# Products of constants, read by nobody, placed in TensorE's waits: routed FFN fronts, experts' first rows, layer 1 and the mixers' fronts

## The chip, the core and the metric

The kernel runs on one core of a Trainium2 chip. The time is device microseconds from start to end of one execution. A profiled execution also gives a trace with a record of each instruction of the engines: TensorE (PE), with its weight loads apart (PEld), VectorE (DVE), ScalarE (ACT), GpSimd (POOL) and SyncE (SP), which issues DMAs here. It also gives PEclk, the clock that the throttle granted to TensorE, as a share of full speed.

## The reference

A net of four layers works on `x` of shape [2, 512, 256] in FP32, that is 1024 tokens of width 256. Each layer is a feed-forward part, a mixing part and a second feed-forward part with the same weights, each added to `x` after a layernorm.

```python
# L0 ffn: 32 experts, top 6, plus a shared expert
scores = softmax(x2d @ wg_router.T); topk_w, topk_idx = top_k(scores, 6)
...
g = einsum('ecd,edf->ecf', xe, w_gate); u = einsum('ecd,edf->ecf', xe, w_up)
ye = einsum('ecf,efd->ecd', silu(g) * u, w_down)
...
return y + silu(x2d @ ws_gate) * (x2d @ ws_up) @ ws_down
```

Layer 0 mixes by retention (followed by an MLP), layer 1 by sparse attention between two binarized linear layers, layer 2 by a Mamba2 block with 8 heads, layer 3 by one with 64 heads. Layer 2's feed-forward part has 8 dense experts, of which each token takes one. Layer 3's is routed like layer 0's, with 8 experts, of which each token takes 2. So the routed feed-forward part runs four times: twice in layer 0, twice in layer 3.

## The kernel before

`x` stays in SBUF as 8 chunks of 128 tokens, four to each half `b`. The stages run one after the other (list at L2083). A tile framework orders the instructions of each engine by a simulated list schedule, and gives PSUM slots out of pools: a tile with the tag `mm` takes a slot of the pool when the earlier owner has been read. `in_order` (L136 to L153) pins the program order of the engines that it names, within its block. What a stage leaves for `x` is added late: `self.pending[b]` holds a function for each chunk, which `settle` calls.

**Routed feed-forward, `moe` (L621 to L722).** The front (L646 to L660) does for each half a layernorm on DVE and GpSimd (L208 to L223), then 8 transposes on PE (`transpose_tokens`, L172 to L178, two PSUM tiles of 512 columns). After both halves come the router's `logits` (L312 to L321: for each chunk two accumulated matmuls of 32 or 8 columns), copied out by DVE at L320; then the scores (L730 to L735 in layer 0, L748 in layer 3), top k and slot lists on DVE (L299 to L307, `slot_lists` L403 to L503). PE and ACT are pinned in the front. The shared expert (`shared_unit`, L355 to L393) follows on PE in the meantime: `pg` and `pu` (L365), `Silu` on ACT (L368), `h` on DVE (L369), the product back (L375) and the addition to `x` (L393).

**Experts, `experts_sparse` (L506 to L616).** The work is a pipeline over units (expert and up to two tiles of 128 rows). GpSimd gathers rows by an indirect DMA (L527), `turn_x` transposes them (L541) and evacuates them into `xeT`, `hidden` multiplies by gate and up (L551, 352 columns) and forms `he` (L555 on ACT, L556 on DVE), `turn_h` transposes (L565), `down_` multiplies (L576), and GpSimd scatters the result to DRAM (L581). A second such loop sits in a branch (L690 to L692) that runs only when an expert has more rows than its tiles; the trace shows it not taken.

**Layer 1 (L1105 to L1440).** A loop at L1301 runs over chunks with stages `front`, `turn_x`, `back`, `measure`, `norm`. `front` begins with the addition of what layer 0 left: six rows per token are read back from DRAM (`add_rows`, L696 to L722) and summed on PE against the identity (L711).

**Mamba, `mamba` (L1567 on).** Its head (L1946 to L2001) pins PE, ACT and DVE. `row(0)` makes the first half's transposed layernorm; in layer 3 it runs chunk by chunk (`by_chunks`, L254 to L276): add the pending rows, normalise one chunk, two transposes (L272). In layer 2, named `few` in the code, the rows are there at once. Then `decay_sums` (L1606 to L1672: `pd` at L1620, row sums `ps_row` L1646, `ps_cum` L1664, `ps_dec` L1669), projections with a convolution (`pp` L1679, ACT L1682, taps on DVE L1686), `products` of B and C (L1703 to L1716) and `prep_back` (L1758 to L1765).

## Time and profile before

| | us |
|---|---|
| median of 3 runs | 2017.6 |
| lowest, highest | 2016.25, 2018.17 |
| the profiled execution | 2018.74 |
| its span, first to last instruction | 2016.9 |
| its mean granted clock of TensorE | 0.923 |

The page's idle times tell for how long an engine stood still before an instruction and which engine's end or DMA released it. For example, the ACT line among the waits

```
ACT s L368 <- PE pg L365: 47.9, 13, 8.8
```

says that ACT stood still before `s` (L368) 13 times for `pg` from PE, 47.9 us in all and 8.8 at the longest. A window line (a stretch in us) gives the busy time and the number of instructions of PE, PEld, DVE, ACT and POOL, then the granted clock, the share of the DMA engines and GB/s. In the slices of the page each digit is a tenth.

TensorE is 87% busy over the span. It stands still at the seams of the stages, where the next layernorm, a gather or rows from DRAM come first.

### The profile page before, as it was taken

How to read it: one execution, taken by the hardware profiler on the slowest of the kernel's cores; microseconds unless marked ns; L12 is line 12 of the kernel's file. 1: busy time of each engine (PE TensorE's matmuls, PEld its weight loads, DVE VectorE, ACT ScalarE, POOL GpSimd, SP SyncE). 2: the span in 40 equal slices, each digit the busy share in tenths (PEclk: the TensorE clock that was granted, in tenths of full speed). 3: DMA queues.
4: the chain of work that ended last, by engine and by line, in shares of the span. 5: the costliest groups of instructions: out<-in, count | busy, mean ns of one | idle time of the engine just before them, and what ended most of it. 6: DMA issues, size and time to landing. Idle time of an engine off the chain costs nothing. (4 is left out here: it accounts for less than half of the span.)

```text
span 2016.9 us, 29547 instructions
## 1 busy us (share of the span) xinstructions
PE 1748.0 (87%) x10566; PEld 1243.7 (62%) x10566; DVE 1145.4 (57%) x2673; ACT 796.8 (40%) x1340; POOL 903.6 (45%) x889
## 2 busy tenths in 40 slices
PE   6899769788999678789788989589999899999885
PEld 4677636465777545454465457357777677777564
DVE  4433276226333376556584643478777787777533
ACT  1123224311233134301661012268777677777111
POOL 3477655310777430100140026136657456767253
PEclk9899989888999889979897989699999999999788
DMA  8266440050556600000230013434454444543133
GB/s 312 82 189 190 147 178 12 11 167 13 170 185 185 214 27 1 2 21 1 95 106 22 3 54 98 137 123 149 152 168 147 147 147 159 172 149 118 44 97 96
DMA packets 117439, 226.47 MB, mean 112 GB/s; under 512 B 22382, under 2 KB 68828, under 8 KB 117014
## 3 DMA queue, kind: packets, MB, share of 16 engines
q1 hardware_dynamic: 88134, 170.17, 25.8%
q0 software_dynamic: 20608, 48.45, 7.5%
q10 hardware_dynamic: 8528, 5.72, 0.9%
q8 instruction: 92, 1.51, 0.3%
q14 instruction: 77, 0.63, 0.1%
HBM read 195.59 MB, written 41.81 MB: 118 GB/s over the span
## 5 line engine op out<-in xcount | busy, mean ns | idle before, releaser
L527 POOL DMA_INDIRECT xe<-table,sl_get x176 | 180.3, 1024 | 211.1 <-DVE sl_get L503 122.0
L551 PE MATMUL ps_gu<-we,xeT 128*128 128x352 f32 x704 | 234.2, 476 | 3.1 <-DVE xeT L130 3.1
L581 POOL DMA_INDIRECT rows<-ye,sl_put x176 | 176.8, 1005 | 82.7 <-issue 41.4
L1686 DVE SCALAR_TENSOR_TENSOR xc<-pp,L_attn_cols,xc 128x511 f32<-128x511 f32 (+2 forms) x216 | 161.4, 747 | 28.7 <-ACT xc L1682 23.4
L576 PE MATMUL ps_ye<-we,hT 88*128 88x256 f32 x704 | 168.1, 379 | 2.9 <-ACT ye L132 1.7
L556 DVE SCALAR_TENSOR_TENSOR he<-se,xe,ps_gu 128x176 f32<-128x176 f32 x176 | 69.9, 397 | 176.1 <-ACT se L555 167.0
L551 PEld LDWEIGHTS ps_gu<-we,xeT 128*128 128x128 f32 x704 | 130.8, 197 | 62.1 <-issue 6.0
L576 PEld LDWEIGHTS ps_ye<-we,hT 88*128 88x128 f32 x704 | 133.4, 190 | 36.5 <-ACT ye L132 3.6
L1813 PE MATMUL pz<-xT,wt 128*128 128x128 f32 x1152 | 143.3, 278 | 12.4 <-ACT xt L1762 6.2
L1789 DVE SCALAR_TENSOR_TENSOR lm<-lm,jb,top 128x128 f32<-128x128 f32 x576 | 153.6, 341 | 0.0
L1679 PE MATMUL pp<-xT,wx 128*128 128x512 f32 x288 | 143.2, 621 | 4.8 <-issue 1.6
L1813 PEld LDWEIGHTS pz<-xT,wt 128*128 128x128 f32 x1152 | 135.9, 193 | 17.8 <-issue 9.3
L555 ACT ACTIVATE se<-ps_gu 128x176 f32<-128x176 f32 x176 | 55.8, 317 | 228.2 <-PE ps_gu L551 228.2
L1898 PE MATMUL yacc<-wt,y 128*128 128x256 f32 x576 | 143.0, 391 | 0.9 <-POOL y L1868 0.6
L1868 POOL TENSOR_TENSOR y<-y,sg 128x512 f32<-128x512 f32 x72 | 91.8, 1274 | 106.3 <-DVE y L1867 104.8
L1806 POOL TENSOR_TENSOR ce<-ce,CT 128x1024 f32<-128x1024 f32 x54 | 127.9, 2369 | 0.0
L1898 PEld LDWEIGHTS yacc<-wt,y 128*128 128x128 f32 x576 | 104.0, 190 | 23.7 <-issue 10.1
L1518 PE MATMUL ps_y<-w8T,xT 128*128 128x512 f32 x256 | 118.4, 617 | 0.0
L1841 PE MATMUL py<-lm,xt 128*64 128x128 f32 x1152 | 108.2, 282 | 10.6 <-DVE lm L1798 3.9
L1798 DVE TENSOR_TENSOR lm<-lm,M 128x1024 f32<-128x1024 f32 x72 | 87.2, 1215 | 46.7 <-ACT lm L1794 44.1
L1879 POOL TENSOR_TENSOR sqs<-sqs,sq 128x512 f32<-128x512 f32 x56 | 71.3, 1274 | 89.0 <-ACT sq L1878 89.0
L217 POOL TENSOR_SCALAR ln_rstd<-ln_mv 128x4 f32<-128x4 f32 x15 | 3.5, 235 | 234.9 <-DVE ln_mv L209 223.7
(402 smaller groups left out, 3465.3 us busy)
## 6 DMA issues: line engine op xcount, KB each, us to landing
lm<-rows SPq DMA_DIRECT2D x72, 512.0 KB
ce<-rows SPq DMA_DIRECT2D x54, 512.0 KB
rows<-zero POOLq DMA_DIRECT2D x16, 768.0 KB, 9.4
y<-rows SPq DMA_DIRECT2D x16, 768.0 KB
we<-in_L_ffn_w_gate_dram SPq DMA_DIRECT2D x64, 176.0 KB
we<-in_L_ffn_w_up_dram SPq DMA_DIRECT2D x64, 176.0 KB
we<-in_L_ffn_w_down_dram SPq DMA_DIRECT2D x64, 176.0 KB
we<-in_L_ffn_w_dram SPq DMA_DIRECT2D x48, 176.0 KB
```

Source lines behind the costliest of these rows:

```text
L527: nc.gpsimd.indirect_dma_start(xe[:, i, :], None, table, bass.IndirectOffsetOnAxis(get[:, e * per + j : e * per + j + 1], 0), bounds_check ...
L551: nc.tensor.matmul(pg, xeT[:, k, i * P : (i + 1) * P], wgu[:, :, k], start=(k == 0), stop=(k == KD - 1))
L576: nc.tensor.matmul(py[:, i, :], hT[:, q, i * P : (i + 1) * P], wd[:, q, :], start=(q == 0), stop=(q == 1))
L581: put_rows = nc.gpsimd.indirect_dma_start(rows, bass.IndirectOffsetOnAxis(put[:, e * per + j : e * per + j + 1], 0), y[:, i, :], None, bou ...
L1518: nc.tensor.matmul(ps, xT[:, k, cs], self.w8T[:, k, 2 * e2 : 2 * e2 + 2, :], start=(k == 0), stop=(k == KD - 1))
L1679: nc.tensor.matmul(pp, wv[:, k, :], xT[:, k, b * S : (b + 1) * S], start=(k == 0), stop=(k == KD - 1))
L1686: nc.vector.scalar_tensor_tensor(out[:, 3 - w :], pp[:, : S - 3 + w], cw[:, m, w : w + 1], out[:, 3 - w :], ALU.mult, ALU.add)
L1789: nc.vector.scalar_tensor_tensor(k["lm"][:, h, :], k["lm"][:, h, :], jb[:, k["c"], n : n + 1], top, ALU.add, ALU.min)
L1806: nc.gpsimd.tensor_tensor(k["ce"], k["ce"], ct, ALU.mult)
L1813: nc.tensor.matmul(pz[:, m, :], u["wz"][:, kk, m * P : (m + 1) * P], xT[:, kk, c * P : (c + 1) * P], start=(kk == 0), stop=(kk == KD - 1),)
L1841: nc.tensor.matmul(py[i * HP : (i + 1) * HP, m, :], w[:, h * HP : (h + 1) * HP], v[:, h, :], start=(m == 0 and n == 0), stop=(n == len(src ...
L1898: nc.tensor.matmul(yacc[cc // 2][:, cc % 2, :], k["y"][:, m, :], u["wo"][:, m, :], start=(u["g"] == 0 and m == 0 and cc % 2 == 0), stop=(u ...
```

## The change

A helper `warm(psum, n)` takes one PSUM tile and multiplies the identity n times by 256 columns of a constant table into it. Nobody reads the tile. The calls, with the number of products:

- `moe` front: 4 ahead of each half, and 1 after each of the first 7 chunks of the logits (15 in each of the four fronts)
- `experts_sparse`: 2 ahead of the transposes of the first unit's rows and 2 after them, in the slot of the second unit's down product (so `down_` now names its tag; the slot is the same)
- `by_chunks`: 1 ahead of each of the first 3 chunks' transposes
- layer 1: 18 ahead of the loop
- `decay_sums(0)`: 4 ahead of the row sums; `products(0)`: 4 ahead; `prep_back` of the first unit, m = 2: 3 ahead
- `mamba` front: 4 in layer 2, 18 in layer 3, ahead of `row(0)`

In the code of the calls that run, this is 60 + 16 + 3 + 18 + 8 + 8 + 6 + 22 = 141 products. The branch of L690 has its own four, which don't run.

```diff
+    def warm(self, psum, n, tag="mm", w=256):
+        ps = psum.tile([P, S], F32, tag=tag, name="warm")
+        for _ in range(n):
+            self.nc.tensor.matmul(ps[:, :w], self.ident, self.c["le"][:, :w], start=True, stop=True)
...
@@ by_chunks
                     self.centre(xn[:, j, :], b * CB + j, *ms[j])
+                    if j < CB - 1:
+                        self.warm(psum, 1)
                     for k in range(KD):
...
@@ logits
-    def logits(self, pool, psum, xT, wT, e):
+    def logits(self, pool, psum, xT, wT, e, warm=False):
...
+            if warm and c < NC - 1:
+                self.warm(psum, 1)
         self.nc.vector.tensor_copy(lg, ps)
...
@@ experts_sparse
         def turn_x(n, xe, nt):
+            if n == 0:
+                self.warm(ps, 2, tag="ps_ye1")
             pt = ps.tile([P, KD, nt * P], F32, name="ps_xe")
...
+            if n == 0:
+                self.warm(ps, 2, tag="ps_ye1")
             xeT = ew.tile([P, KD, nt * P], F32, name=f"xeT{n % 2}")
...
-            py = ps.tile([P, nt, D], F32, name=f"ps_ye{n % 2}")
+            py = ps.tile([P, nt, D], F32, tag=f"ps_ye{n % 2}", name=f"ps_ye{n % 2}")
...
@@ moe
                         for b in range(B):
+                            self.warm(psM, 4)
                             xn = lp.tile([P, CB, D], F32, name=f"xn{b}")
...
-                        s = self.logits(sb, psM, xT, rT, E)
+                        s = self.logits(sb, psM, xT, rT, E, warm=True)
...
@@ l1
             with tc.tile_pool(name="a1m", bufs=4, space=PSUM) as psM:
+                self.warm(psM, 18)
                 for c in range(NC + 4):
...
@@ mamba: decay_sums, products, prep_back, head
                 yield
+                if b == 0:
+                    self.warm(psM, 4)
...
             def products(b):
+                if b == 0:
+                    self.warm(psM, 4)
...
             def prep_back(u, m):
+                if u["b"] == u["g"] == 0 and m == 2:
+                    self.warm(psM, 3)
...
             with self.in_order(tail, ("PE", "Activation", "DVE")):
+                self.warm(psM, 4 if few else 18)
                 row(0)
```

## The prediction

> **What bounds the kernel now.** I read the busy shares first, then the slices with the granted clock, then windows of 3.41 us, then the timeline around each place that the change touches.

> From the page, parts 1 and 2:

> ```profile
> PE 1748.0 (87%) x10566; PEld 1243.7 (62%) x10566; DVE 1145.4 (57%) x2673; ACT 796.8 (40%) x1340; POOL 903.6 (45%) x889
> ...
> PE   6899769788999678789788989589999899999885
> ...
> PEclk9899989888999889979897989699999999999788
> ```

> TensorE is the bound over the whole, but with gaps at the seams between stages, and behind the gaps the granted clock falls. The mean clock is 0.923; since the record only ever shows 1.0 and 0.5, about 15% of the span, some 310 us, is at half clock, much of it idle. The change can only win where matmuls run at half clock on the path.

> Next, windows that follow the clock's own grid (columns: stretch in us; busy us and instruction count of PE, PEld, DVE, ACT, POOL; granted clock; DMA share; GB/s):

> ```profile
> 441.84:445.25 3.41, 2.16 (x8) 1.48 (x8) 2.53 (x9) 0.00 (x0) 0.74 (x1) 0.50 0.09 33
> 452.08:455.50 3.42, 3.42 (x18) 3.42 (x18) 0.00 (x0) 0.88 (x1) 0.00 (x0) 0.50 0.60 207
> 458.91:462.32 3.41, 3.41 (x5) 1.35 (x4) 1.64 (x11) 1.61 (x2) 0.00 (x0) 0.50 0.00 0
> 462.32:465.74 3.42, 3.42 (x9) 1.52 (x8) 2.51 (x13) 0.60 (x1) 0.00 (x0) 1.00 0.00 0
> 503.28:506.70 3.42, 1.19 (x6) 0.63 (x5) 2.24 (x6) 0.00 (x0) 2.70 (x3) 1.00 0.72 211
> 506.70:510.11 3.41, 2.63 (x6) 1.54 (x6) 2.33 (x4) 0.00 (x0) 2.60 (x3) 0.50 0.45 137
> ```

> Busy time does not lift the clock: the second window is 100% busy with router logits (32 columns each) and stays at half; one window of 512-column matmuls (458.91) lifts it. In the fifth, PE is busy 1.19 of 3.42 us and the clock falls at its end. I counted, for every window of the trace, the share in which columns stream (columns times 1.67 ns at half clock: 256 columns take 0.427 us there and 0.216 at full). Of windows at half clock those at 0.61 to 0.64 stayed, 0.71 and 0.75 mostly rose; of those at full clock, the ones below about 0.3 mostly fell, those from 0.35 up mostly stayed.

> Then the timeline (start, us, engine, line, operation, out<-in, count, idle before and its releaser):

> ```profile
> 449.92 6.88 PE L317 MATMUL ps_lg<-routerT,xT 128*128 128x32 f32 x32
> 456.61 3.76 PE L365 MATMUL pg<-xT,wsh 128*128 128x512 f32 x4
> 463.23 0.69 DVE L369 SCALAR_TENSOR_TENSOR h<-s,pu 128x512 f32<-128x512 f32 x1 [2.58 <-PE pu L365]
> ...
> 506.30 0.72 PE L541 MATMUL ps_xe<-cst,xe 128*128 128x128 f32 x3 [0.92 <-DMA xe<-table,sl_get]
> 507.81 5.06 PE L551 MATMUL ps_gu<-we,xeT 128*128 128x352 f32 x8 [0.78 <-DVE xeT L130]
> ...
> 1161.09 4.09 PE L317 MATMUL ps_lg<-routerT,xT 128*128 128x8 f32 x32
> ...
> 1278.08 0.66 PE L272 MATMUL ps_tr<-cst,xn 128*128 128x128 f32 x2 [13.24 <-DVE xn L198]
> 1283.90 3.68 PE L1620 MATMUL pd<-wb,xT 128*128 128x64 f32 x16 [0.57 <-DVE xT L130]
> ```

> A front (449.92) runs logits and its first 512-column products at half clock, and DVE then waits for them. The first expert's matmul (507.81) takes 5.06 us; the same eight instructions at 519.95 take 2.53. Layer 3's mixer idles 13.24 us and starts cold.

> [...] the clock changes only at multiples of 3.41 us. [...] window 441.84 (8 transposes, 2.16 us busy) stayed at 0.50. [...] the trace has two instructions for each matmul call (32 for the 16 calls of the logits), so I count one added product as two instructions of 256 columns.

> **The change part by part.** It removes nothing and adds 141 executed products = 282 instructions: 60.9 us of PE at 0.216, 120 us at 0.427. Each site is worth what it shortens behind it, less what it delays. Waits for a PSUM slot I put at nothing: no reader holds a product's tile, the logits hold one of the four slots while the products rotate over the other three, the chunks of the mixer's front hold two, and the slot that the first rows take is not used before the second unit's down product. If such a wait came, it would stand in PE's queue ahead of the transposes or logits; a product ahead of it lasts 0.43 to 0.86 us, so that is its bound per site.

> *First expert rows* (four times: two products before the transposes of x, two after). Layer 0: the first gather waits leave PE near idle, and the evacuation gap (0.78 us) holds two products (0.86) almost entirely. If the clock stays up, the eight instructions take 2.53 instead of 5.06: +2.95 us in the first, +2.8 in the second call. GpSimd, whose gathers and scatters run nearly without pause there (4 x 1.32 us a unit against PE's 5.0), has caught up with 4.9 us to spare by the loop's end, so the gain passes through. Layer 3: PE waits 5.06 us for the gather (1198.98), longer than a window, and two products fill only 0.86 of it; eight instructions from 1200.87 at 0.62 each; I take +0.8 each (-0.3 to +1.4), because with more columns in the window the clock should rise 3.4 us earlier in part of the phases. Sum +7.3.

> *Routed fronts* (4 before each half, 7 between the logits). Logits at full clock with 14 product instructions: 32 x 0.107 + 14 x 0.216 = 6.4 us; at half: 32 x 0.215 + 14 x 0.427 = 12.9. At half clock logits with products stream columns for 0.62 (layer 0) or 0.53 (layer 3) of the time, below what lifts it, so the four products before the halves must have lifted it. Layer 0, second: 8 x 0.427 = 3.4 us of products just ahead of the cold transposes; if lifted, logits last 6.4 instead of 6.9, pg and pu 3.4 instead of 6.3, DVE's waits of 2.58 and 0.73 go: +4.0; if not, -5.5. At 0.75: +1.5. Layer 0, first: ScalarE's Exp waits for a DMA until 34.19 while the logits are copied at 27.27, so that wait covers 5.5 us of lengthening; without that cover -4. I take -0.4. Layer 3, first: halves back to back from 1157.62, no gap for anything, and the clock is already up for most of it: 8 x 0.216 + 14 x 0.216 = +4.7 us of work, of which some 2 lies in DVE's waits: -2.5 (-1.3 to -6). Layer 3, second: logits cold (6.83): +2.2 if lifted, -6 if not: +0.2. Sum -1.2.

> *Layer 1* (18 products = 7.8 to 15 us before the loop). The y rows land at 686.05, PE idles 12.9 us before; the adds at 686.16 (5.22 us, half clock) would be faster, but DVE is busy to 691.39 anyway and PE idle again to 694, which drops the clock: 0 (±1).

> *Layer 2's mixer.* The clock is full there (pd 2.10): the front's four cost -0.5 to -1.7; those ahead of the row sums and of the B and C products keep the clock in a stretch where it falls (970.9 to 974.3): +0.5 to 1.5 and +1.0; the three in m=2 about -0.2. Net +1 (±1.5).

> *Layer 3's mixer.* 18 products, about 9.7 us, run in the 13.24 us idle; three more between chunks (idle 0.5 to 1.4). pd then takes 1.7 to 2.1 instead of 3.68 (the price at 946.95, layer 2, full clock), pp 3.43 instead of 5.84; ScalarE's first use of pp (1291.13) comes some 3.4 earlier. Row sums and B/C products +2.1, m=2 -0.3; but DVE's taps are queued there in a fixed order and may take 0.5 of it: +4.7 (±2).

> Sum: 7.3 - 1.2 + 0 + 1 + 4.7 = +11.8; I take 11 for small waits of PSUM slots and the scheduler's changed order, which no row shows. The profiled execution is 2018.7 us (span 2016.9 and 1.8 outside), 1.1 above the median of 2017.6. 2018.7 - 11 = 2007.7, from the median 2006.6; I take 2007.5.

> **Rivals.**
> A (0.48), the sum above: 2001 to 2013.
> B (0.10), every front lifts: first rows 7.3, fronts +4.0 + 2.2 - 1.3, mixers 2.5 and 6.7, layer 1 +1: 22.4, so 1996. For it: PE waits for DVE before the halves. Against: the layer 3 front has no gap.
> C (0.18), no change (2014 to 2021): products issue as soon as their PSUM slot is free, so they run at the start of an idle and the clock falls again before the work. For it: 18 products take 9.7 of 13.24 us, and GpSimd or DVE may pace the loop anyway. It takes away most of layer 1, of the mixer and of layer 3's first rows, leaving the two layer 0 rows (5.8) against the fronts' certain cost (4).
> D (0.24), slower: logits with products between them are caught at half clock. Place: the fronts of layer 0 (second) and of both layer 3 halves. Price: 14 x 0.427 = 6.0 us each plus up to 3.4 for the block between halves. For it: two of three are wholly cold now, and 0.53 to 0.62 cannot lift. Against: eight instructions of 256 columns ahead of them. It decides once three fronts fail: -18 and -4 more for the first, against +12: 2022 to 2029.

> **How the numbers follow.** The likeliest is A: 2007.5, its own range 2001 to 2013. To hold 8 in 10 the range reaches into B, over C and half of D: 1999 to 2023. A change under 0.2% (4 us) cannot be told from none here. Faster by more: A and B, 0.58; within: C, 0.18; slower: D, 0.24.

> **What would show it.** First rows of layer 0 at 2.5, not 5.06 us; logits at 6.4, not 12.9; pd of layer 3's mixer at about 2 us and ScalarE's first use of pp 3 us sooner after the last transposes; DVE's 2.58 gone; the mean clock above 0.94. It is wrong if PE reaches the logits at half clock in two of the fronts, if the 18 products end more than 3.4 us ahead of the transposes, or if the rows' gain comes back as a longer wait for gathers in the same loop.

## The result and the profile after

The changed kernel took 1999.2 us (median of 4 runs, 1997.7 to 2002.2) against 2017.6 before: ratio 0.9911, 95% interval [0.9894, 0.9929], or 18 us less. Compared again, with 25 runs of before beside four of its own (experiment e5 below), it came to 0.9890 [0.9875, 0.9905]. The prediction, 2007.5 with 1999 to 2023, had the direction, and the time lies just inside its lower end, but it had only a little over half of the gain. The profiled execution is the slowest of the four, 2002.15 us, with a span of 2000.2.

The page of the changed kernel, parts 1 and 2:

```profile
PE 1780.3 (89%) x10848; PEld 1277.8 (64%) x10848; DVE 1145.9 (57%) x2673; ACT 796.4 (40%) x1340; POOL 903.1 (45%) x889
...
PE   6999859899999878789788999789999899999895
...
PEclk8999979899999889979897999899999999999998
```

282 instructions more, 32 us more PE busy time, and yet a shorter span: the mean clock went from 0.923 to 0.946, and the time at half clock from 311 to 216 us (own sum over the clock's record).

To see where the time went, I matched every instruction of the two traces by engine, line and tile, and took the difference of their end times at the stages' ends. It is a sum of my own, not a view of the profile (us, changed less before; negative is gained):

| stretch of before's trace | step | predicted |
|---|---|---|
| layer 0, first front (0 to 72) | +2.1 | +0.4 |
| first rows there (72 to 83) | -2.8 | -2.9 |
| rest to the second front (83 to 443) | +2.6 | 0 |
| layer 0, second front (443 to 501) | -5.9 | -1.5 |
| first rows there (501 to 513) | -2.4 | -2.8 |
| layer 1 and layer 2's mixer with its sides (513 to 1154) | -1.4 | -1 |
| layer 3, first front and rows (1154 to 1206) | -1.0 | +1.7 |
| layer 3's mixer, head (1206 to 1330) | -4.3 | -4.7 |
| layer 3's mixer, rest (1330 to 1874) | +5.3 | 0 |
| layer 3, second front and rows (1874 to 1937) | -9.8 | -1.0 |
| to the end | +0.8 | 0 |

Three lines of it are far from the prediction: the second fronts of both layers, and the rest of layer 3's mixer. Two more are off by some 2.7 us, the stretch from 83 to 443 us and layer 3's first front with its rows.

The timeline of the changed kernel, layer 0's second front and first rows (start, us, engine, line, operation; L164 is the product, L326 the logits, L376 pg and pu, L566 gate and up):

```profile
442.69 1.99 PE L164 MATMUL warm<-cst 128*128 128x256 f32 x8
...
446.59 1.89 PE L164 MATMUL warm<-cst 128*128 128x256 f32 x8
...
450.99 0.53 PE L326 MATMUL ps_lg<-routerT,xT 128*128 128x32 f32 x4
451.36 0.68 PE L164 MATMUL warm<-cst 128*128 128x256 f32 x2
...
457.51 1.96 PE L376 MATMUL pg<-xT,wsh 128*128 128x512 f32 x4
...
503.90 2.63 PE L566 MATMUL ps_gu<-we,xeT 128*128 128x352 f32 x8
```

The products ran at full clock (8 in 1.9 us), the logits with their products took 6.6 us from 450.99, pg 1.96 instead of 3.76, and the eight first gate and up instructions 2.63 instead of 5.06. This is the successful case of the prediction's step.

The timeline of VectorE in layer 3's second front, before and then changed:

```profile
1901.50 0.68 DVE L369 SCALAR_TENSOR_TENSOR h<-s,pu 88x512 f32<-88x512 f32 x1 [2.47 <-PE pu L365]
1902.10 0.21 DVE L308 TENSOR_TENSOR tk_eq<-tk_eq,tk_cum 128x64 f32<-128x64 f32 x1
1904.93 0.68 DVE L369 SCALAR_TENSOR_TENSOR h<-s,pu 88x512 f32<-88x512 f32 x1 [2.61 <-PE pu L365]
1905.54 0.21 DVE L309 TENSOR_TENSOR tk_gt<-tk_gt,tk_eq 128x64 f32<-128x64 f32 x1
```

```profile
1891.17 0.68 DVE L380 SCALAR_TENSOR_TENSOR h<-s,pu 88x512 f32<-88x512 f32 x1 [0.91 <-PE pu L376]
1891.78 0.21 DVE L317 TENSOR_TENSOR tk_eq<-tk_eq,tk_cum 128x64 f32<-128x64 f32 x1
1892.03 0.23 DVE L318 TENSOR_TENSOR tk_gt<-tk_gt,tk_eq 128x64 f32<-128x64 f32 x1
...
1894.61 0.68 DVE L380 SCALAR_TENSOR_TENSOR h<-s,pu 88x512 f32<-88x512 f32 x1
```

Before, the second `h` stood ahead of `tk_gt` in VectorE's order and the whole of the slot lists waited 2.61 us behind it for TensorE. In the changed kernel it stands behind the start of the slot lists and waits for nothing. Nobody wrote that order. It came out of the list schedule, presumably because that counts the products as work of TensorE ahead of `pu`. The same swap is in layer 3's first front. So there are two theories for the fronts: clock, and order.

In layer 0's second front VectorE takes `h` in the order of before, so what is won there is not the order's. In layer 0's first front the order changed, and there it hurts. VectorE's `h` and TensorE's product that waits for it, before and then changed:

```profile
36.56 0.68 DVE L369 SCALAR_TENSOR_TENSOR h<-s,pu 128x512 f32<-128x512 f32 x1
37.29 2.00 PE L375 MATMUL acc<-wsh,h 128*128 128x256 f32 x8 [0.56 <-DVE h L369]
```

```profile
39.35 0.66 DVE L380 SCALAR_TENSOR_TENSOR h<-s,pu 128x512 f32<-128x512 f32 x1
40.08 3.78 PE L386 MATMUL acc<-wsh,h 128*128 128x256 f32 x8 [4.26 <-DVE h L380]
```

The first `h` is queued behind further steps of top k (`tk_gt` to `tk_cum`) here, so the product back starts 2.8 us later. TensorE, done with pg and pu before that, waits 4.26 us instead of 0.56, its clock falls at 38.3, and the product takes 3.78 instead of 2.00 us. The scores' Exp on ScalarE came only 0.7 us later (34.86 against 34.19).

### The profile page after: what moved, and what is told of

It reads as the page before. It is cut to its first block, busy times and chain, and to the rows that moved or that the text cites. A ratio compares the mean times of both kernels' runs of the same rounds, so it can differ in the third digit from the quotient of the medians.

```text
span 2000.2 us, 30117 instructions
## 1 busy us (share of the span) xinstructions
PE 1780.3 (89%) x10848; PEld 1277.8 (64%) x10848; DVE 1145.9 (57%) x2673; ACT 796.4 (40%) x1340; POOL 903.1 (45%) x889
## 5 line engine op out<-in xcount | busy, mean ns | idle before, releaser
L566 PE MATMUL ps_gu<-we,xeT 128*128 128x352 f32 x704 | 224.6, 460 | 0.0
L566 PEld LDWEIGHTS ps_gu<-we,xeT 128*128 128x128 f32 x704 | 126.3, 190 | 55.4 <-DVE xeT L130 1.3
L1698 PE MATMUL pp<-xT,wx 128*128 128x512 f32 x288 | 138.7, 605 | 4.8 <-issue 1.2
L1921 PEld LDWEIGHTS yacc<-wt,y 128*128 128x128 f32 x576 | 104.2, 190 | 24.2 <-issue 10.3
```

Source lines behind the costliest of these rows:

```text
L566: nc.tensor.matmul(pg, xeT[:, k, i * P : (i + 1) * P], wgu[:, :, k], start=(k == 0), stop=(k == KD - 1))
L1698: nc.tensor.matmul(pp, wv[:, k, :], xT[:, k, b * S : (b + 1) * S], start=(k == 0), stop=(k == KD - 1))
L1921: nc.tensor.matmul(yacc[cc // 2][:, cc % 2, :], k["y"][:, m, :], u["wo"][:, m, :], start=(u["g"] == 0 and m == 0 and cc % 2 == 0), stop=(u ...
```

## The experiments

All times are compared with runs of before on the same chip. Of one kernel they scatter by some 10 us (53 runs of before on one chip: 2016.3 to 2025.7), so the intervals matter more than a single trace.

**e1, the experts' first rows alone.** Against the changed kernel, all sites but `turn_x` are taken out:

```diff
-                            self.warm(psM, 4)
...
-                        s = self.logits(sb, psM, xT, rT, E, warm=True)
+                        s = self.logits(sb, psM, xT, rT, E)
...
-                self.warm(psM, 18)
...
-                self.warm(psM, 4 if few else 18)
```

and likewise in `by_chunks`, `decay_sums`, `products` and `prep_back`.

> Only the products of the experts' first rows (2 ahead, 2 after, in four loops). By the prediction's terms: 7.3 us less than before, 2010.3 (2.9 in each layer 0 loop, 0.8 in each of layer 3). By the sum read off the changed kernel's trace: 10.3 us less, 2007.3 (2.8, 2.7, 1.9, 2.9). Rival, that the loops' gain comes back as longer waits for gathers: under 3 us. In layer 0 the first eight ps_gu instructions take 2.5 instead of 5.06 us by every theory but the rival's.

Measured: 0.9992 [0.9981, 1.0004], no difference that can be told. Yet locally it does what was said. The timeline of this kernel:

```profile
503.65 1.03 PE L164 MATMUL warm<-cst 128*128 128x256 f32 x4
504.59 2.63 PE L564 MATMUL ps_gu<-we,xeT 128*128 128x352 f32 x8
```

By the matched traces it won 2.8, 2.6 and 2.7 us in three of the four loops and nothing in layer 3's first (where the whole change won 1.9), and lost 5.2 us in layer 1 and 3.4 in layer 3's first front, where it has no product. The runs fell into two groups, 6 of 22 at 2010 to 2013 and the others at 2018 to 2026; the trace, at 2019.3, is of the second group, so what the first group did not lose is not seen.

**e2, the four fronts alone.** The same, but the front's two lines stay and `turn_x` loses its own:

```diff
         def turn_x(n, xe, nt):
-            if n == 0:
-                self.warm(ps, 2, tag="ps_ye1")
...
-            if n == 0:
-                self.warm(ps, 2, tag="ps_ye1")
```

> Only the products of the four routed fronts. By the prediction's terms: a loss of about 1 us, 2018 to 2019. By the changed kernel's trace: 10 us less, 2007 to 2008 (first front of layer 0 +2, second -6, first of layer 3 about 0, second -7). The order of VectorE's work differs from before here as it does in the whole change: in layer 3 the second h of the shared expert goes behind the slot lists' first part.

Measured: 0.9967 [0.9956, 0.9977], 6.6 us less. In its trace it won 5.9 in layer 0's second front and 7.6 in layer 3's second with the rows behind it, and lost 3.3 in layer 0's first; but layer 3's mixer, which it doesn't touch, took 5.4 us longer.

**e3, the mixers alone**: `by_chunks`, `decay_sums`, `products`, `prep_back` and the mixers' fronts keep theirs.

```diff
-                self.warm(ps, 2, tag="ps_ye1")
...
-                            self.warm(psM, 4)
...
-                        s = self.logits(sb, psM, xT, rT, E, warm=True)
+                        s = self.logits(sb, psM, xT, rT, E)
...
-                self.warm(psM, 18)
```

> Only the products of the two mixers (fronts, chunks, row sums, B and C products, m = 2). By the prediction's terms: 5.7 us less, 2012. By the changed kernel's trace: layer 2 0.4, and in layer 3 4.1 us won by the head, of which 5 were lost again in two windows of the body that the clock lost there: between 2012 and 2018, depending on whether those windows fall so again. The instruction order is that of before, so any gain here is the clock's.

Measured: 1.0020 [1.0012, 1.0028], slower. **e7, layer 3's mixer alone**, is that kernel with layer 2's products off as well:

```diff
-                if b == 0:
+                if b == 0 and not few:
                     self.warm(psM, 4)
...
-                self.warm(psM, 4 if few else 18)
+                if not few:
+                    self.warm(psM, 18)
```

and likewise in `prep_back`.

> Only layer 3's mixer: 18 products ahead, 3 between chunks, row sums, B and C products, m = 2; none in layer 2. By the prediction: 4.7 us less (0.9977). By the traces so far, which win 4 to 6 us by the head and lose 4 to 5 of it in the body: 0.999 to 1.001. If the loss of 4 us of the mixers' kernel comes from here: 1.002.

Measured: 0.9984 [0.9975, 0.9993]. Layer 2's mixer itself was 0.2 us shorter in e3 than in e7, and layer 3's differs by 0.3 in the sum of its head and body. What differs is a place that neither touches, layer 3's first front. Timeline of e3, then of e7:

```profile
1155.86 3.67 PE L184 MATMUL ps_tr<-cst,xn 128*128 128x128 f32 x16
1159.33 6.83 PE L326 MATMUL ps_lg<-routerT,xT 128*128 128x8 f32 x32
1166.02 3.69 PE L376 MATMUL pg<-xT,wsh 128*88 128x512 f32 x4
```

```profile
1155.98 3.67 PE L184 MATMUL ps_tr<-cst,xn 128*128 128x128 f32 x16
1159.44 4.08 PE L326 MATMUL ps_lg<-routerT,xT 128*128 128x8 f32 x32
1163.38 3.32 PE L376 MATMUL pg<-xT,wsh 128*88 128x512 f32 x4
```

The same instructions within 0.1 us of the same time since the start, but the clock's windows (the 3.41 us stretches of the grid on which it changes) lie otherwise: I took the time from the last window edge to this front's start (0.2 us ahead of its first transpose), 2.01 us in e3 and 2.24 in e7. In all traces with neither products nor a pinned order here the outcome goes with it: at 2.06 us or less (e1, e3, e9) the stretch to the slot lists' end took 3.4 to 3.5 us longer than before's, at 2.19 and 2.24 (before, e7) 0.0. The two with the pinned order of e4 and no products here split in the same way, 3.5 us apart (e8 at 1.75, e4 at 2.24). The last section counts what stood in two of those windows. With all the front's products (changed, e2, e5, e6, e10, e12, at 1.83 to 2.33 us) it took 0.6 to 0.9 us longer at any phase: a small loss against a good phase, some 2.6 us won against a bad one. So a part's worth depends on what the other parts do to the phase.

**e4, the order alone, no product.** The edit, with `late` given for layer 3 only:

```diff
+                late = nc.vector.tensor_scalar(m, m, scale, None, ALU.mult).ins
...
+            if late is not None and half == 0 and len(hs) == 2:
+                self.tc.add_manual_dep(
+                    i.ins,
+                    late.name,
+                    mybir.DependencyInfo(mybir.DependencyClass.NoSync, mybir.DependencyReason.DATA),
+                    reason="in_order",
+                )
```

> No product at all; in layer 3's two fronts the shared expert's second h is queued on VectorE behind the weights' last scaling (as the changed kernel's schedule has it). Theory order: VectorE no longer waits 2.6 us for that h ahead of the slot lists, so 2.6 + 0.7 us in each of the two fronts, 6.6 us less, 2011. Theory clock (the fronts' gain is from the clock alone): no change, 2017.6 +- 1.5.

Measured: 0.9976 [0.9963, 0.9988], 4.9 us less, between the two but far from none. Its VectorE timeline in layer 3's second front shows what the swap leaves:

```profile
1899.59 0.68 DVE L379 SCALAR_TENSOR_TENSOR h<-s,pu 88x512 f32<-88x512 f32 x1 [2.25 <-PE pu L375]
...
1905.49 0.17 DVE L455 TENSOR_REDUCE sl_full<-ps_pos 128x1 f32<-128x8 f32 x1 [2.50 <-PE ps_pos L446]
```

The first `h` still waits, at half clock, and VectorE waits 2.50 for `ps_pos` on TensorE, which stands behind other work there. From the copy of the logits to the end of the slot lists each of layer 3's fronts won 1.9 and 2.3 us by the order alone, 5.9 and 5.9 in the whole change. So the order without the clock is worth a third to two fifths of it. The reverse, the products with the order of before, was not run, so how much of the rest needs the order is open.

**e5, the whole change again**, with no edit.

> The whole change again, beside many runs of before. If the parts add up (first rows 0.9992, fronts 0.9967, mixers 1.0020): 0.998, 4 us less. If the first comparison of four runs each holds: 0.991, 18 us less. The second would mean that the parts help one another[...].

Measured: 0.9890 [0.9875, 0.9905]. The parts do not add: 4 us by their sum, 22 together.

**e6, the whole change without the mixers' products.**

```diff
-                if b == 0:
-                    self.warm(psM, 4)
...
-                if u["b"] == u["g"] == 0 and m == 2:
-                    self.warm(psM, 3)
...
-                self.warm(psM, 4 if few else 18)
```

> The whole change without the mixers' products (fronts, first rows and layer 1 stay, with the whole change's order of VectorE and TensorE). If the mixers' products cost 4 us as they did alone: faster than the whole change by 0.2%. By the prediction's terms (mixers +5.7 us): slower than the whole by 0.3%.

Measured: 0.9904 [0.9889, 0.9919], inside the interval of e5. Beside e5's own runs on the same chip it is slower: its four took 2000.0 to 2003.9 us, e5's four 1995.5 to 2000.0, and the medians are 3.2 us apart. So the mixers' products, which cost 4 us alone, do not cost here and seem to win some 3; with four runs each that is not sure. In the two traces the difference stands in layer 2's mixer: 2.5 us lost in e6, 0.4 won in e5.

**e8, what the traces' terms say is best**: rows, the fronts' products in each layer's second call only, and e4's pinned order.

```diff
-                            self.warm(psM, 4)
+                            if self.calls in (2, 4):
+                                self.warm(psM, 4)
...
-                        s = self.logits(sb, psM, xT, rT, E, warm=True)
+                        s = self.logits(sb, psM, xT, rT, E, warm=self.calls in (2, 4))
```

> First rows, the fronts' products only in the second call of each layer, the pinned order of h in both of layer 3's fronts, nothing in the mixers and layer 1. By the traces' terms against the whole change: first front of layer 0 spares 2.5, first of layer 3 spares 2.4 us, mixers spare 4: 9 us faster than the whole. If the clock decides in all fronts and mixers alike, it is slower than the whole by 5 us or more.

Measured: 0.9905 [0.9888, 0.9921], not told apart from the whole change, and not 9 us faster. The sum over local terms failed again: in its trace it lost 2.1 us in layer 1 and 2.5 in layer 2's mixer, which have no products in it.

The last four runs fell on chips on which before takes 2105 and 2107 us, since every expert loop lasts 8 to 38 us longer than in before's trace. Only ratios are used of them, and they are no measure against e5.

**e9, first rows and layer 1**, which is e1 with one line put back.

```diff
+                self.warm(psM, 18)
                 for c in range(NC + 4):
```

> The experts' first rows and layer 1's 18 products, nothing else. The first rows alone came to 0.9992, and their profiled run lost 5.2 us in layer 1 that kernels without the rows' products did not lose. If layer 1's products keep the clock there whatever the phase (theory: parts help one another): 0.996, 8 us less. If the parts add and layer 1's are worth nothing, as the prediction has it: 0.999.

Measured: 0.9976 [0.9958, 0.9995], between the two. Layer 1 lost nothing in its trace (-0.3), in layer 2's mixer it lost 2.5, in layer 3's first front 3.5.

**e10 and e12, the whole change without the products of layer 0's first front.**

```diff
-                            self.warm(psM, 4)
+                            if self.calls > 1:
+                                self.warm(psM, 4)
...
-                        s = self.logits(sb, psM, xT, rT, E, warm=True)
+                        s = self.logits(sb, psM, xT, rT, E, warm=self.calls > 1)
```

> The whole change without the products of layer 0's first front. By the traces that front loses 2.1 to 2.6 us by its products: 2 to 3 us faster than the whole change, 1995 to 1996 by the whole's 1998. If only the phase of the clock's windows decides what is left over, no difference from the whole.

> The kernel without the products of layer 0's first front once more, since the chip of its first comparison ran every expert loop 8 to 35 us longer (before at 2105 us) and the whole change was not run beside it. If the chip has before near 2018 to 2020: a ratio 0.0013 below the whole's 0.989 to 0.991 (2.6 us spared in that front), so 0.988 to 0.990, if the sum holds; equal to the whole's or above, if what is spared there is taken by the windows' phase in the stages behind.

Measured: 0.9922 [0.9892, 0.9952] and 0.9929 [0.9907, 0.9951]. Whether leaving that front out helps stays open. But e12 told something: with the same code, layer 1 was 0.7 us shorter than before's in e10 and 4.8 longer in e12, both with layer 1's 18 products. They are no sure protection of layer 1, then.

**e11, the products between the logits taken out in all four fronts**, with e4's pinned order.

```diff
-                        s = self.logits(sb, psM, xT, rT, E, warm=True)
+                        s = self.logits(sb, psM, xT, rT, E)
```

> The whole change without the products between the logits, in all four fronts, with layer 3's order of h pinned as the whole has it. Theory clock: logits without products let the clock fall, pg and pu run at half again, 3 us lost in layer 0's second and layer 3's second front, against 3 us of products saved in each of the other two: near the whole's time (+-2). Theory order (the logits' products matter for the scheduler's order alone): 3 us saved in each of the four, 10 us faster than the whole.

Measured: 0.9947 [0.9927, 0.9968], beside 0.9922 for e10 on the same chip; the intervals overlap. It is not faster than e10, which speaks against the theory that they matter for the order alone. Its timeline in layer 0's second front:

```profile
483.44 3.66 PE L326 MATMUL ps_lg<-routerT,xT 128*128 128x32 f32 x32
486.93 3.66 PE L377 MATMUL pg<-xT,wsh 128*128 128x512 f32 x4
```

The logits alone run at full clock (3.66 us against 6.88 in before; the eight products ahead already do, at 1.89), and under them it falls (the record has half clock from 487.0 to 490.5): pg is at half clock again. What the seven products cost, about 3 us, they bring back and a little more: this front won 5.0 us in e11 and 5.9 in e10, layer 3's second front with its rows 9.1 and 9.8.

## Why the prediction was right, and where it was too small

The measured 1999.2, and e5's 1998.0, lie outside the range that the likeliest case A gave itself (2001 to 2013) and nearest to rival B's 1996, which had a chance of 0.10. B's premise came true, that the clock is up in the fronts; its larger gains in the mixers did not. That the sum lies inside the whole range is in part luck, since terms that were far off stand against each other: the fronts won more, the mixer's body and the stretch from 83 to 443 us lost what nobody had counted.

- **First rows, +7.3.** Layer 0's came about as worked out: 2.95 and 2.8 predicted (2.53 of it for the eight instructions; the working doesn't show the rest), 2.8 and 2.4 won in the changed kernel's trace, the second 2.7 if it is read 2 us later, when all engines show it. Of the first, the phase owns some: without these products the stretch was 1.1 to 1.4 us shorter than before's in e2, e3 and e4 too, and not in e7. Nothing came back in the loops (their steps are 0.0 and -0.3). Layer 3's were mis-sized: 0.8 taken for each, 1.9 and 2.9 won in the whole change, 0.1 and 2.7 in e1.
- **Routed fronts, -1.2.** This is the step that failed. In layer 0's second front the good case came true in every trace that had products there: 5.0 (e11, the blocks alone) to 5.9 us won, of which before's own trace owns about 1.9 (four kernels without products there won that as well, at another phase), so the +4.0 of the good case. The case of a front stuck at half clock, -5.5, showed in no run, and averaging it in made +1.5 of it. In layer 3's second front the working priced only the clock and came to +0.2; the slot lists ended 6.9 us earlier (6.9 to 7.3 in all seven traces with all its products). Layer 3's first front cost 0.7, not 2.5. The shares worked out for logits caught at half clock, 0.62 and 0.53, come to 0.60 and 0.50 by their own terms, which changes nothing in the argument.
- **"small waits of PSUM slots and the scheduler's changed order, which no row shows"** was put at a loss of 0.8 in the sum. In layer 3 the order was instead worth 4.9 us alone (e4), and with the second `h` out of the way nothing on VectorE waits for it at its old place; in layer 0's first front it delayed `h`. Over the whole the sign was wrong.
- **Layer 0's first front, -0.4**: 2.1 and 2.6 us lost in the two traces of the whole change, 3.3 and 4.1 in e2 and e6, which have the same products there; 0.3 to 1.4 in the kernels without on chips of the same speed. The cover of ScalarE's wait held to within 0.7 us; the rest lies behind the first `h`, which VectorE takes later, as shown above; TensorE waits 3.2 to 6.4 us for it in all four traces and then runs at half clock. In e11 the order there is before's, the product starts at 37.65, and it is at half clock all the same (3.78 us); that front lost 1.6 us, on a slower chip. So the order and the clock both cost here, and how much each is not separated.
- **Layer 1, 0, and layer 2's mixer, +1**: layer 1 (read to layer 2's router) was 0.5 to 0.7 us shorter in the two traces of the whole change, as in kernels without its products (0.5), and layer 2's mixer 0.2 to 0.4. Right for the first; the second is small in these traces, but e6, e8 and e9, without its products, lost 2.5 us there, and e12 lost 3.3 with them.
- **Layer 3's mixer, +4.7.** The head won 4.3 us, though not where I said: pd still ran at half clock (3.68 us) in the changed kernel's trace, and ScalarE's first use of pp came 0.8 us sooner after it, not 3.4. Some 3 us came later, between 1300 and 1316 of before's time, at the row sums and the B and C products. Then the body took all of it back. ScalarE's waits for the output weights (total, times, longest), before and changed:

```profile
ACT wt L1753 <- DMA wt<-n_L_attn_out_proj_w_dram: 19.4, 7, 3.9
```

```profile
ACT wt L1774 <- DMA wt<-n_L_attn_out_proj_w_dram: 23.2, 7, 5.1
```

  Over thirteen traces (before, changed, e1 to e11) the two go together: bodies that took 0 to 0.4 us more than before's have waits of 19.0 to 19.8 us, those that took 3.6 to 6.0 more have 21.6 to 24.9, and three between (e4, e7, e8) took 1.7 to 3.0 more with 19.4 to 20.9. One place shows how a wait becomes a loss, before and then changed:

```profile
1476.22 0.51 ACT L1753 ACTIVATE wt<-wt,L_attn_cols 128x256 f32<-128x256 f32 x1 [3.39 <-DMA wt<-n_L_attn_out_proj_w_dram]
1477.89 2.03 PE L1813 MATMUL pz<-xT,wt 128*128 128x128 f32 x16
```

```profile
1467.18 0.51 ACT L1774 ACTIVATE wt<-wt,L_attn_cols 128x256 f32<-128x256 f32 x1 [5.06 <-DMA wt<-n_L_attn_out_proj_w_dram]
1469.18 3.26 PE L1836 MATMUL pz<-xT,wt 128*128 128x128 f32 x16
```

  ScalarE waits 1.7 us longer, TensorE behind it stands idle for 2.23 us instead of 0.56, the clock is at half from 1468.5 for one window, and `pz` takes 3.26 instead of 2.03: 3.2 us lost. Of the thirteen traces besides before's, the ten whose bodies took 1.7 us or more longer have half clock in a window of the body where before has none; e1, e6 and e9 have only before's one, at 1606. That is a match, not a proof: the transfer was not moved alone. e2 has 23.9 without any product in the mixer, so it is not the head's lead alone.
- **Rival D**, logits caught at half clock with their products between, did not occur: in the changed kernel's trace they took about 6.6 us in layer 0's second and layer 3's first front (from 450.99 and from 1157.41), not 12.9. **Rival C's** mechanism, products that end too early, showed in layer 3's mixer: 38 product instructions ran from 1259.81 to 1270.2, four more stood between the transposes until 1272.0, and the clock fell again at 1273.9. Layer 1's 36 ended at 681.6, with the adds behind them at 2.75 instead of 5.22 us; then TensorE was idle again and the clock fell at 686.8, as the prediction had it.

What is not settled is why the parts do not add. Stage by stage, I set the steps of e1, e2 and e3 together against those of the changed kernel and of e5 (us, single traces): layer 1 +4.2 against -0.8 and -0.5; layer 3's first front +7.6 against 0.7 and 0.6; its first rows +0.8 against -1.9 and -2.2; the body of layer 3's mixer +11.7 against 5.3 and 3.6; the other way, layer 0's second front -9.5 against -5.9 twice, since the phase of before's trace is counted three times there. That is the size of the gap between 4 and 22. For layer 3's front the phase explains it (e1, e3 and e7), and there the whole change's products take the phase out. For layer 1 and the mixer's body it is likely but not shown, and e12 shows that having products in layer 1 does not always keep it.

## What to carry to other kernels

- A dummy product pays where it stands ahead of wide matmuls that would start cold and that somebody waits for: behind a gather (the first gate and up instructions of layer 0's second loop took 2.63 instead of 5.06 us), or ahead of and between logits (pg behind them took 1.96 us in layer 0's second front; with none between the 32-column logits of e11 the clock fell under them and pg took 3.66). It must keep columns streaming up to them: in layer 3's mixer the last product was done at 1272.0, the clock fell at 1273.9, and pd behind it still took 3.68 us.
- Adding work to an engine changes a list schedule's order on the others. Compare the orders first: here a third or more of a gain in two fronts was the place of one instruction on VectorE, and it can be had without any product, while in another front the new order made TensorE wait longer.
- The clock changed here only on a grid of 3.41 us, and the stages of each kernel lay otherwise against it (layer 3's first front 2.01 us behind an edge in e3, 2.24 in e7): a part measured alone moves every stage behind it against the windows. Judge by many runs of the whole, not by the sum of parts or one trace.

## What the runs showed of the hardware that was not expected

The cliff also bears on the prediction's window at 441.84, which stayed at half clock with eight transposes. The window over the transposes of layer 3's first front, in before and in e3:

```profile
1158.64:1162.05 3.41, 3.41 (x19) 3.41 (x17) 1.38 (x2) 1.17 (x2) 1.74 (x4) 0.50 0.02 5
1157.06:1160.47 3.41, 3.41 (x18) 3.41 (x17) 1.34 (x2) 1.17 (x2) 1.56 (x4) 0.50 0.00 0
```

TensorE is busy throughout in both, with nothing but 128-column transposes and the first 8-column logits. By the prediction's measure (128 columns at 1.67 ns are 0.213 us) columns stream for 0.74 of the first window, in which eleven transposes start, and for 0.69 of the second, with ten. After the first the clock rose; after the second it stayed at half. Of the seven traces without products there, the three at 0.74 and 0.75 rose (before, e4, e7) and the four at 0.62 to 0.70 did not (e1, e3, e8, e9). So the clock did rise here after windows of hardly anything but transposes, at 0.74 and 0.75; the eight transposes at 441.84 are only 0.50 of theirs. Counted so over all fourteen traces, no window at half clock below 0.69 lifted it, and none at full clock below 0.35 kept it.
